# Linear attention with a mixture of experts: moving VectorE work behind the scaling of y, spreading attention to tile 129, and turning the rows of tiles 14 to 26 by transfers

## The chip, the cores and the metric

One core of a Trainium2 chip runs the whole kernel. TensorE (PE in the profile), VectorE (DVE), ScalarE (ACT), GpSimd (POOL) and SyncE (SP) each work through their own queue in order; SP, ScalarE and GpSimd also start DMA transfers. The metric is the device time of one execution in microseconds (us). Shown times are medians of several executions; the profile is of one execution.

## The reference, cut to what matters

x has 8 sequences of 1024 rows of 256 float32. The rows are layer-normalised (xn), and two things are added to x:

```
q = elu(xn @ Wq.T) + 1;  k = elu(xn @ Wk.T) + 1;  v = xn @ Wv.T        # 16 heads of 16
kv_cumsum = cumsum over rows of k outer v;  k_cumsum = cumsum over rows of k
out = (q . kv_cumsum) / clip(q . k_cumsum, 1e-6)                       # causal, per head
attention = out @ Wo.T

logits = xn @ Wr + br;  the best two of 8 experts, softmax over the two
ffn = sum over the two experts of weight * (silu(xn @ W1[e]) * (xn @ W3[e])) @ W2[e]

result = x + attention + ffn
```

W1 and W3 are 256 x 512 for each expert, W2 is 512 x 256. All arithmetic that goes to the result is float32.

## The kernel before, in words

**Two streams of work.** The 8192 rows are 16 blocks of 512 rows (`NBLK`), each of four chunks of 128. Attention goes block by block. The experts work on tiles of 128 gathered rows of one expert each: 132 tiles (`NM`), of which the first 25 (`N1`) come from lists made of the first four blocks (`FB`), the others from lists made of all blocks (`second_batch`). After a setup of some 47 us the main loop calls `tile_step(j)` for j = 0 to 132; each call does one expert tile and, spread between, a few steps of attention, normalisation, routing and list making.

**Order.** In the main loop only TensorE's order is written out by hand (`tc.manual_schedule(engines={EN.PE})`). What VectorE, ScalarE and GpSimd do next is set by the framework's planner when the kernel is built: it takes what it reckons to be ready, earlier program text first. `in_order` fixes the order of single instructions on their engine (the SP transfers, some ScalarE work), and `tc.issue_after(ins)` puts instructions of the same engine as `ins`, traced within it, behind `ins`.

**An expert tile** (`ffn_step`, line 1429). `ffn_weights(j + 2)` (line 1365) loads W1 and W3 of the tile two ahead, 512 KB each, on SP. `ffn_hidden(j)` (line 1378) multiplies by W1 (16 matmuls, called the gate here), calls `between`, multiplies by W3 (16 matmuls), then ScalarE applies silu and VectorE multiplies (hT). Then the rows of tile j + 1 are turned, then `ffn_out(j - 1)` (line 1405) does the 8 matmuls with W2 for the tile before, and VectorE scales the result by the routing weight into y (line 1417). `ffn_store` (line 1419) has GpSimd add y to the result rows by an indirect DMA. Such stores, and the accumulating transfers of attention (line 1099), read and write the output, so each waits for the landing of the one before.

**Turning rows.** Gathered rows (xg) are normalised by `ffn_norm` on ScalarE and must be transposed before the gate. Tiles below `TURNED` go through TensorE: `ffn_turn` (line 1344), two 128x128 transposes into PSUM and a ScalarE copy, one tile ahead. The others are normalised two tiles ahead; `ffn_halves` (line 1317, VectorE) splits the floats into 16-bit halves, `ffn_turn_halves` (line 1324) has SP start a transposing transfer between the two weight loads, and `ffn_join` (line 1334, ScalarE) puts the halves together, one tile ahead. Before, `TURNED` is 27.

**Attention.** `block_steps` (line 1106) is a generator with 8 steps a block: projections of k, q and v (0 to 2), divisors and the scores of chunk 0 (3), and one step for each chunk (4 to 7). In a chunk's step `attend` (line 1083) multiplies the last chunk's outcome (oT) by Wo, `carry` (line 1024) multiplies q by the running state, `scores` (line 1003) computes the next chunk's scores, which VectorE masks (line 1018), and `weigh` (line 1037) adds the scores' part and makes the new state: VectorE writes oT (line 1065), the new product (line 1068) and adds the old state (line 1077). `attend_upto(n)` (line 1145) advances the steps to n, of 129 (`LAST`); `upto` in `tile_step` says how far tile j may go. From tile 22 (`READ`) on it rises evenly, to reach 129 at tile 121 (`END`).

**Tiles 1 to 11 also prepare a block each** (block t = 4 + j). `turn(t)` (line 348) transposes block t between gate and W3; `logits(t)` follows the outputs. `normalise(t + 1)` (line 330, ScalarE, four activations) comes at the end of the tile in `finish`. It needs `stats` (line 298: VectorE, four pairs of operations on a block) and `deviations` (line 307: 17 small VectorE operations, each on the one before, for two blocks at a time). Both are called early in the tile, before `ffn_step`, two blocks ahead. Every fourth block `route` (line 417) chooses experts and counts (`counting`, tiles 4, 8 and 12; the counts are the matmuls of line 483).

**Tiles 14 to 21 also make the second lists**: in each, five calls `piece(0)` to `piece(4)` advance `second_batch` (line 741) by a `one_hot` (VectorE lines 606 and 619, ScalarE lines 624 and 626), four matmuls (line 771) and sums (line 780).

**PSUM.** y, the divisors, the outputs of `attend` and the lists' sums share two buffers (`ps_y`); scores, gate and W3 products share four (`ps_mm`).

Of the kernel before, what the change touches and what calls it, by code (L numbers as in the profile page):

```python
# [51 lines left out]
ALU = mybir.AluOpType  # L52
# [12 lines left out]
def tile_attention_moe(  # L65
# [14 lines left out]
    nc = tc.nc  # L80
# [5 lines left out]
    NCH = TB // P  # L86
# [7 lines left out]
    FB = 4  # L94
# [209 lines left out]
    def moments_tile(n):  # L304
        return f_two.tile([P, n * NCH, 2], F32, tag="mv", name="mv")
# [800 lines left out]
    def block_steps(t):  # L1106


        yield from project(t)
        denominators(t)  # L1110
        if t + 1 < NBLK:
            fetch(t + 1)
        waiting = scores(t, 0)
        if behind:
            attend(*behind.pop())
        yield
        done = None
        for c in range(NCH):
            if done:
                attend(*done)  # L1120
            both_ps = carry(t, c)
            coming = scores(t, c + 1) if c + 1 < NCH else None
            oT = weigh(both_ps, *waiting)
            done = t, c, oT
            waiting = coming
            yield
        behind.append(done)
        if t + 1 == NBLK:
            attend(*behind.pop())
            yield  # L1130
# [274 lines left out]
    def ffn_out(j, last=False):  # L1405
        hT = hs.pop(j)
        e = expert_of(j, mybir.EngineType.PE)
        y_ps = ps_y.tile([P, H], F32, tag="y", name="y_ps")
        for i in range(IC):
            done = nc.tensor.matmul(  # L1410
                y_ps, lhsT=hT[:, i, :], rhs=w2_sb[:, bass.ds(e * (IC * H) + i * H, H)],
                start=(i == 0), stop=(i == IC - 1),
            )
            if last:
                in_order(done)
        ys[j] = ffn5.tile([P, H], F32, tag="y", name="y")
        nc.vector.tensor_scalar(ys[j], y_ps, entry.pop(j)[:, 0:1], None, ALU.mult)  # L1417

    def ffn_store(j):
        _, _, _, _, rows, dst_i, i = of_tile(j)  # L1420
# [30 lines left out]
                stored[0] += 1  # L1451


    TURNED = 27
    gathered = ffn_load(0)
    with tc.issue_after(gathered.ins):
        in_order(nc.gpsimd.tensor_copy(te_late, batches[0][1]))
# [14 lines left out]
                nc.sync.dma_start(out=wo_sb, in_=woT.rearrange("(k p) o -> p k o", p=P))  # L1472
            )
    LATE = 3
    END = NM - 11
    LISTS = NBLK - FB
    READ = LISTS + 10
    AHEAD = 2 + LISTS // 2 + READ - LISTS
    held = {}

    def tile_step(j):
        nonlocal routing
# [8 lines left out]

        def piece(place):
            if LISTS + 2 <= j < READ or (j, place) == (READ, 0):
                next(held["lists"])

        def between():
            if turning:
# [14 lines left out]
        def finish():  # L1512
            if turning:
                held["lgT"] = f_two.tile([P, P], F32, tag="lgT", name="lgT")
                nc.scalar.copy(held["lgT"], logits(t))
            if counting:
                next(routing)
            if t + 1 < NBLK:
                normalise(t + 1)

        if LISTS <= j < LISTS + NBLK - FB:
# [3 lines left out]
        if j < LISTS:  # L1525
            upto = 3 + j // 2
        elif j < READ:
            upto = AHEAD - (READ - j - 1)
        else:
            upto = AHEAD + (LAST - AHEAD) * (j - READ + 1) // (END - READ + 1)  # L1530
        waits = attend_upto(upto, put_off=True)
        if t <= NBLK:
            with tc.issue_after((last_token if j < 3 else last_masked)[0].ins):
# [8 lines left out]
                if counting:  # L1542
                    routing = route(t - ROUND, t)
                    next(routing)
                of_blocks = [] if j == 0 else [t + 1, t + 2] if j == 1 else [t + 2]
                for a in of_blocks:
                    if a < NBLK:
                        if a % 2 == FB % 2:
                            held["mv"] = moments_tile(2)
                        some = slice(0, NCH) if a % 2 == FB % 2 else slice(NCH, 2 * NCH)  # L1550
                        stats(a, held["mv"][:, some])
                        if a % 2 != FB % 2:
                            deviations(a - 1, 2, held.pop("mv"))
        piece(1)
        ffn_step(j, LATE if N1 < j <= N1 + LATE else 0, between, after, late, finish)
        piece(4)
# [74 lines left out]
```

## Time and profile before

| | |
|---|---|
| median of 12 executions | 1249.22 us (1246.66 to 1253.48) |
| profiled execution, its own time | 1248.42 us |
| its span | 1246.7 us |
| TensorE busy | 1193.9 us (96%) |
| VectorE busy | 686.2 us (55%) |
| ScalarE busy | 588.5 us (47%) |
| GpSimd busy | 549.9 us (44%) |
| moved by DMA | 252.68 MB, mean 203 GB/s |
| transposing transfers of rows | 105 |

How to read it: "busy" is the time in which an engine carried out instructions; TensorE's has its pipelined matmuls modelled. A line such as `L1417 DVE ... y<-y_ps,entry` names the code line, the engine, what is written and what is read. "PEclk" is the TensorE clock that was granted, as a share of full speed. `xN` counts instructions. "idle before <-releaser" is how long the engine stood still before an instruction and whose end let it go; where several things were waited for, it is the last that the profile sees. In the table by stretches the columns are: the stretch, its length, then busy time and instruction count of PE, PE's weight loads, DVE, ACT and POOL, then PEclk, the DMA share and GB/s. In the table of waits the three figures are total us, number of times and the longest.

### The profile page before, as it was taken

The page shows a single profiled execution, that of the slowest core. Times are in us where ns is not written, and L with a number is a line of the kernel's source. Part 1 is how long each engine was busy: PE and PEld are TensorE (multiplying, and loading weights), DVE is VectorE, ACT ScalarE, POOL GpSimd, SP SyncE. Part 2 cuts the span into 40 slices and gives each one's busy share as a digit, 9 for nine tenths or more (in the row PEclk, how much of TensorE's full clock was granted, in tenths as well). Part 3 has the DMA queues.
Part 4 walks back from the last instruction along what each step waited for, and adds up shares of the span by engine and source line. Part 5 has one row for each costly group of instructions (what it writes and reads, how often), then busy time and mean ns, then how long its engine had stood idle before and what let it go on. Part 6 is the DMA issues. An engine that isn't in the chain of part 4 may idle for free. (4 is left out here: it accounts for less than half of the span.)

```text
span 1246.7 us, 29841 instructions
## 1 busy us (share of the span) xinstructions
PE 1193.9 (96%) x11394; PEld 1049.6 (84%) x11394; DVE 686.2 (55%) x1537; ACT 588.5 (47%) x1098; POOL 549.9 (44%) x474
## 2 busy tenths in 40 slices
PE   8799998899999999999999999999999999999992
PEld 6688887778989898989888889898988888888992
DVE  7866669755455555454555555555536464646320
ACT  5655576592363535352727262626272626262230
POOL 4734343325444544444444444444445444444342
PEclk9989999999999999999999999999999999999996
DMA  9898667557898988889898989898999798988992
GB/s 327 310 290 241 183 204 211 140 165 198 185 242 199 192 214 182 202 193 228 183 218 173 218 174 210 183 210 183 204 191 230 162 226 169 225 169 208 196 241 26
DMA packets 232463, 252.68 MB, mean 203 GB/s; under 512 B 101474, under 2 KB 156386, under 8 KB 232034
## 3 DMA queue, kind: packets, MB, share of 16 engines
q1 hardware_dynamic: 189298, 198.61, 56.8%
q0 software_dynamic: 38272, 43.22, 25.0%
q10 hardware_dynamic: 4752, 8.91, 2.1%
q8 instruction: 94, 1.54, 0.5%
q14 instruction: 47, 0.39, 0.1%
HBM read 187.91 MB, written 44.29 MB: 186 GB/s over the span
## 5 line engine op out<-in xcount | busy, mean ns | idle before, releaser
L1391 PE MATMUL gu_ps<-xgT,w 128*128 128x128 f32 x4224 | 505.7, 277 | 1.8 <-ACT xgT L1352 0.9
L1391 PEld LDWEIGHTS gu_ps<-xgT,w 128*128 128x128 f32 x4224 | 491.0, 193 | 17.2 <-issue 10.0
L1421 POOL DMA_INDIRECT out_dram<-y,dst_i x107 | 173.8, 1624 | 311.7 <-DVE s_sb L1018 76.6
L1410 PE MATMUL y_ps<-w_sb,hT 128*128 x1056 | 250.8, 380 | 1.7 <-DVE hT L1402 0.9
L1297 POOL DMA_INDIRECT xg<-in_x_dram,src_i x132 | 135.2, 1024 | 193.6 <-DVE half L1320 87.6
L1399 ACT ACTIVATE hT<-gu_ps 128x512 f32<-128x512 f32 x132 | 79.3, 601 | 290.6 <-PE gu_ps L1391 280.2
L1410 PEld LDWEIGHTS y_ps<-w_sb,hT 128*128 128x128 f32 x1056 | 190.4, 190 | 23.8 <-issue 1.8
L1018 DVE TENSOR_TENSOR s_sb<-s_ps,causal 128x512 f32<-128x512 f32 x256 | 158.3, 680 | 75.3 <-PE s_ps L1011 75.3
L1402 DVE TENSOR_TENSOR hT<-gu_ps,hT 128x512 f32<-128x512 f32 x132 | 90.4, 685 | 59.4 <-PE gu_ps L1391 43.6
L1302 POOL DMA_INDIRECT entry<-tab_d,of_i x107 | 108.6, 1015 | 32.6 <-issue 32.0
L1320 DVE COPY half<-xg 128x512 uint16<-128x512 uint16 x105 | 47.0, 447 | 133.4 <-ACT xg L1310 133.4
L1417 DVE TENSOR_SCALAR y<-y_ps,entry 128x256 f32<-128x256 f32 x132 | 63.6, 482 | 98.0 <-PE y_ps L1410 94.7
L1096 ACT COPY at<-a_ps 128x256 f32<-128x256 f32 x64 | 23.8, 372 | 167.6 <-PE a_ps L1091 167.6
L1310 ACT ACTIVATE xg<-xg,entry 128x256 f32<-128x256 f32 x132 | 79.0, 600 | 8.0 <-DMA entry<-tab_d,of_i 4.9
L1338 ACT COPY xgT<-halfT 128x512 uint16<-128x512 uint16 x105 | 80.2, 764 | 3.4 <-DMA halfT<-half 3.4
L1011 PE MATMUL s_ps<-qm,kT 32*128 32x256 f32 x1024 | 75.6, 408 | 0.0
L1091 PE MATMUL a_ps<-wo_sb,oT 128*128 128x256 f32 x256 | 68.1, 388 | 6.1 <-DVE oT L1065 4.1
L1421 POOL DMA_INDIRECT acc_d<-y,src_i x25 | 43.6, 1742 | 59.1 <-DVE y L1417 22.3
L1048 PE MATMUL o_ps<-s_sb,va 128*32 128x128 f32 x2048 | 69.4, 276 | 0.0
L1048 PEld LDWEIGHTS o_ps<-s_sb,va 128*32 128x32 f32 x2048 | 52.2, 110 | 18.2 <-issue 16.2
L1091 PEld LDWEIGHTS a_ps<-wo_sb,oT 128*128 128x128 f32 x256 | 46.1, 190 | 18.3 <-DVE oT L1065 5.1
L1099 POOL DMA_DIRECT2D out_dram<-at x27 | 35.9, 1328 | 56.0 <-DMA out_dram<-y,dst_i 21.9
(236 smaller groups left out, 1417.2 us busy)
## 6 DMA issues: line engine op xcount, KB each, us to landing
w<-in_w_dram SPq DMA_DIRECT2D x264, 512.0 KB
rden<-over SPq DMA_DIRECT2D x128, 64.0 KB
xnT<-xnT_d SPq DMA_DIRECT2D x15, 512.0 KB
out_dram<-at POOLq DMA_DIRECT2D x27, 256.0 KB
out_dram<-in_x_dram SPq DMA_DIRECT2D x12, 512.0 KB
xnT_d<-xnT ACTq DMA_DIRECT2D x11, 512.0 KB
xb<-in_x_dram SPq DMA_DIRECT2D x9, 512.0 KB
w_sb<-in_w_dram SPq DMA_DIRECT2D x4, 1024.0 KB
```

Of the source, the lines that this page charges most:

```text
L1018: last_masked[0] = nc.vector.tensor_tensor(sm, s_ps[r].rearrange("p k a l -> p (k a) l"), causal_b, ALU.mult)
L1048: nc.tensor.matmul(o_ps[32 * r : 32 * r + 32, hh, :], lhsT=va[:, c, 4 * hh + r, a, :], rhs=s_sb[r][:, 2 * hh + a, :], start=(first and a = ...
L1091: nc.tensor.matmul(a_ps, lhsT=oT[:, hh, :], rhs=wo_sb[:, hh, :], start=(hh == 0), stop=(hh == 1),)
L1297: rows = nc.gpsimd.indirect_dma_start(out=xg[j], out_offset=None, in_=x_rows[:, :], in_offset=bass.IndirectOffsetOnAxis(ap=src_i[:, i : i ...
L1302: nc.gpsimd.indirect_dma_start(out=entry[j], out_offset=None, in_=table[:, :], in_offset=bass.IndirectOffsetOnAxis(ap=num_i[:, i : i + 1], ...
L1310: nc.scalar.activation(xg[j], xg[j], AF.Identity, bias=entry[j][:, 1:2], scale=entry[j][:, 2:3])
L1338: nc.scalar.copy(xgT[j].bitcast(U16).rearrange("p k (l b) -> p b k l", b=2), halves.pop(j).rearrange("p (b k) l -> p b k l", b=2),)
L1391: done = nc.tensor.matmul(ps[:, i, :], lhsT=w13[:, k, bass.ts(i, P)], rhs=xgT[j][:, k, :], start=(k == 0), stop=(k == KC - 1),)
L1399: silu = nc.scalar.activation(hT, gu[0], AF.Silu)
L1402: nc.vector.tensor_tensor(hT, gu[1], hT, ALU.mult)
L1410: done = nc.tensor.matmul(y_ps, lhsT=hT[:, i, :], rhs=w2_sb[:, bass.ds(e * (IC * H) + i * H, H)], start=(i == 0), stop=(i == IC - 1),)
L1421: nc.gpsimd.indirect_dma_start(out=rows[:, :], out_offset=bass.IndirectOffsetOnAxis(ap=dst_i[:, i : i + 1], axis=0), in_=ys.pop(j), in_off ...
```

## The change

Four things are altered.

1. `TURNED` becomes 2 + 16 - 4 = 14: tiles 14 to 26 are turned by transposing transfers, as those from 27 on.
2. The VectorE instruction that scales y is kept in `held_y`. Every call that advances the second lists is put behind the latest one. So are the deviations, which move from before `ffn_step` to `finish` (tiles 1, 3, 5, 7, 9), and the statistics that used to be taken early in tiles 4 and 8 and the second of the two in tile 1; those move to `finish` as well. The other statistics stay early.
3. In a chunk's step `carry` comes before `attend`.
4. `upto` rises from tile 22 so as to reach 129 at tile 129 (`NM` - 3) instead of 121; `END` is gone.

```diff
         for c in range(NCH):
+            both_ps = carry(t, c)
             if done:
                 attend(*done)
-            both_ps = carry(t, c)
             coming = scores(t, c + 1) if c + 1 < NCH else None
...
-        nc.vector.tensor_scalar(ys[j], y_ps, entry.pop(j)[:, 0:1], None, ALU.mult)
+        held_y[0] = nc.vector.tensor_scalar(ys[j], y_ps, entry.pop(j)[:, 0:1], None, ALU.mult)
+
+    held_y = [None]
...
-    TURNED = 27
+    TURNED = 2 + NBLK - FB
...
-    END = NM - 11
...
+    def take_stats(t):
+        second = t % 2 != FB % 2
+        if not second:
+            held["mv"] = moments_tile(2)
+        stats(t, held["mv"][:, second * NCH : (second + 1) * NCH])
...
         def piece(place):
             if LISTS + 2 <= j < READ or (j, place) == (READ, 0):
-                next(held["lists"])
+                with tc.issue_after(held_y[0].ins):
+                    next(held["lists"])
...
             if t + 1 < NBLK:
+                if j > 0:
+                    with tc.issue_after(held_y[0].ins):
+                        if t + 2 < NBLK and (counting or j == 1):
+                            take_stats(t + 2)
+                        if t + 2 < NBLK and t % 2 != FB % 2:
+                            deviations(t + 1, 2, held.pop("mv"))
                 normalise(t + 1)
...
-            upto = AHEAD + (LAST - AHEAD) * (j - READ + 1) // (END - READ + 1)
+            upto = min(LAST, AHEAD + (LAST - AHEAD) * (j - READ + 1) // (NM - 2 - READ))
...
-                of_blocks = [] if j == 0 else [t + 1, t + 2] if j == 1 else [t + 2]
-                for a in of_blocks:
-                    if a < NBLK:
-                        if a % 2 == FB % 2:
-                            held["mv"] = moments_tile(2)
-                        some = slice(0, NCH) if a % 2 == FB % 2 else slice(NCH, 2 * NCH)
-                        stats(a, held["mv"][:, some])
-                        if a % 2 != FB % 2:
-                            deviations(a - 1, 2, held.pop("mv"))
+                if t + 2 < NBLK and j > 0 and not counting:
+                    take_stats(t + 1 if j == 1 else t + 2)
```

## The prediction

> **What bounds the kernel now.** I read the page first: engine shares, then the 40 slices.
>
> ```profile
> PE 1193.9 (96%) x11394; PEld 1049.6 (84%) x11394; DVE 686.2 (55%) x1537; ACT 588.5 (47%) x1098; POOL 549.9 (44%) x474
> ...
> PE   8799998899999999999999999999999999999992
> ```
>
> TensorE is busy without a break from about 300 us to 1225 us at a granted clock of 1.00; there only removed matmuls help. Time can come from two other places: the waits before 300 us, and the last slice. The waits of TensorE, longest in total first:
>
> ```profile
> PE den L980 <- DVE y L1417: 4.8, 2, 3.6
> PE a_ps L1091 <- DVE oT L1065: 4.1, 3, 2.6
> PE cnt_ps L483 <- DVE mv L302: 3.7, 2, 2.0
> PE a_ps L1091 <- DVE y L1417: 1.9, 2, 1.0
> ```
>
> Each is VectorE doing something else first (block statistics, list pieces). Some cost more than their length. In the table by stretches (TensorE busy is the second figure, the granted clock the third from the end) the stretch after the 2.01 us wait at 134.6 has clock 0.59, the one after the 2.64 us wait at 219.7 has 0.72:
>
> ```profile
> 56.00:60.00 4.00, 3.29 (x33) 2.53 (x32) 4.00 (x26) 0.64 (x2) 2.41 (x3) 1.00 1.08 364
> ...
> 135.00:137.00 2.00, 2.00 (x11) 1.93 (x11) 1.70 (x11) 1.68 (x2) 1.70 (x2) 0.59 0.33 39
> ...
> 220.00:226.00 6.00, 6.00 (x82) 4.70 (x81) 3.23 (x7) 0.79 (x2) 1.77 (x2) 0.72 0.22 27
> ```
>
> The timeline of the end shows the second place: the last output is scaled at 1225.45, but GpSimd still owes four stores, one after another:
>
> ```profile
> 1225.45 0.48 DVE L1417 TENSOR_SCALAR y<-y_ps,entry 128x256 f32<-128x256 f32 x1 [2.09 <-PE y_ps L1410]
> 1225.71 1.55 POOL L1421 DMA_INDIRECT out_dram<-y,dst_i  x1 [3.89 <-issue]
> 1230.22 1.55 POOL L1421 DMA_INDIRECT out_dram<-y,dst_i  x1 [2.96 <-issue]
> 1234.81 1.55 POOL L1421 DMA_INDIRECT out_dram<-y,dst_i  x1 [3.04 <-DMA out_dram<-y,dst_i]
> 1239.32 1.55 POOL L1421 DMA_INDIRECT out_dram<-y,dst_i  x1 [2.96 <-issue]
> ```
>
> The span ends at 1246.7, 21.2 us after that scaling. Stores into the output wait for each other.
>
> **A. Rows of tiles 14 to 26 turned by transfers.** Removed: 13 pairs of transposes. A pair costs TensorE the time from its start to the next matmul's:
>
> ```profile
> 302.82 0.38 PE L1348 MATMUL xg_t<-ident,xg 128*128 128x128 f32 x2
> ...
> 303.04 1.89 PE L1410 MATMUL y_ps<-w_sb,hT 128*128 x8
> ```
>
> 0.22 us, so 13 x 0.22 = 2.9 us gained. Moved: ScalarE joins (0.764) instead of copying (0.365), 0.40 more per tile, 5.2 in all; VectorE gets a split copy of 0.447 each, 5.8 in all; SP issues 13 transposes of 1.2 to 2.1 us between the two weight loads of a tile. Cover: a transfer starts two tiles ahead, some 20 us, and weights come as early. The cover is thinnest for tile 25: its expert is known only when the lists are done, and after the score-divisor transfers its weight loads leave SP at 300.18 with four more behind them, while its first matmul runs at 309.61. How slow a transpose can be in such a crowd, the trace shows once:
>
> ```profile
> 332.46 1.45 SPq L1329 DMA_TRANSPOSE halfT<-half  x1
> ...
> 343.15 0.77 ACT L1338 COPY xgT<-halfT 128x512 uint16<-128x512 uint16 x1 [3.44 <-DMA halfT<-half]
> ```
>
> 10.7 us. Issued near 301.5, tile 25's would land between 304 and 312 and be joined 0.8 later: loss 0 to 3, taken 1. The VectorE and ScalarE cover in the list tiles is counted in C. A: +1.9 (range -0.5 to +3).
>
> A rule stands against this part. The Trainium skill ("VectorE: DVE Perf Modes", section "Rules for kernel authors") says to turn a 128x128 block on TensorE where PSUM will do, and by DMA otherwise; its section "The three transpose paths" has 390 ns against 1309 ns. If that difference were paid in full for 13 tiles (an estimate from these two figures: 12 us), the total below would become about 6 us slower than before. The trace's rows price TensorE at 0.11 us per turned block and show 105 later tiles whose transfers made it wait 0.3 us once, so I go by the rows.
>
> **B. Statistics and deviations (tiles 1 to 11).** In tiles 4 and 8, where routing runs, a block's statistics (4 x 0.57 = 2.3 us) move behind the scaling of y; in tiles 1, 3, 5, 7, 9 the chain of deviations (17 dependent operations, 0.2 us apart, 3.4 us) does. Gained: the waits of the counts, 1.65 in tile 4 and 2.01 in tile 8; behind the latter 16 gate matmuls took 3.30 instead of 1.95 and five others 0.6 longer, so 3.9 together; two waits for logits behind a late y, 1.3. Sum +6.9. The 3.58 us before the divisors of tile 2 I count as nothing: VectorE is busy 4.00 of 4.00 us there, its work stays, and the wait moves to the gate matmuls or the turn of block 6.
>
> What is late next: normalising a block (2.08 on ScalarE) needs the deviations, and TensorE turns it after the next tile's gate matmuls, with the whole in-order queue (second half, outputs) behind. From the scaling of y: 0.4 + 3.4 + 2.1 = 5.9 us. From there to the turn the trace has 127.25 - 121.04 = 6.2 in tile 8 and 108.08 - 101.87 = 6.2 in tile 6 (just enough; 0.8 for both, as the masking of scores, 4 x 0.62, starts to interleave), 149.03 - 143.90 = 5.1 in tile 10 (short by 0.8, with interleaving 1.4), 87.20 - 82.58 = 4.6 in tile 4 (short by 1.3; the masks are ready 1.6 us after y and, taken in between, add 2.5; I take 3 and 1 for the clock). Tile 2: 0.5. Sum -6.7. B: 0. Bounds: no interleaving and tile 2 gaining 1.3 gives +6; interleaving everywhere, the clock falling in two tiles, -8.
>
> The Trainium skill ("TensorE: Matmul & The Clock Gate", section "HAM oscillation — how this bites in real kernels") warns only of idle gaps longer than 3.4 us. By that rule the 2.01 us gap would cost itself alone and B would come to -0.9; the row has clock 0.59 after it.
>
> **C. List pieces behind y, carry before attend (tiles 14 to 22).** VectorE scales y 0.9 to 1.2 us earlier. The waits it holds: 1.19 (divisors), 0.97 (list fill), 2 x 0.97 (outputs); of these 3.8 go, also because the carried product (0.61) now fills the wait for the free PSUM buffer. In tile 17 TensorE waits 2.64 for oT; y and oT could come 1.9 earlier, but the product that now goes first needs the new state, two operations (0.84) later: +1.5 with the clock. Against it: the next list piece starts after y, so its matmuls can wait on VectorE and ScalarE (2 x 1.25 of pieces behind 2.42 of masks): I take 2.5 once; and the 0.45 + 0.40 per tile from A fall where VectorE is busy 11.4 of 12 and ScalarE 26.4 of 29 us: 1.3, plus 0.5 for the 1.48 wait on ScalarE that is there now. C: +1.0. Bounds: all 9.2 us of waits there gone but 3, +6; every tile paying 0.6 for the order, -5. From tile 23 on the state is ready long before the next step, and the swapped order costs nothing; if it were not, 0.84 per step.
>
> **D. Attention up to tile 129.** TensorE's work is the same and it never idles, so its end does not move by this. What moves is the chain of stores. Call T the start of the tile with the last two steps: 1159.9 now (tile 121), tile 129 then. Around T one output store leaves at T - 7.8, then an accumulation, an output, the last accumulation, and the outputs of tiles 128 to 131. Start-to-start times: an output store beside weight loads 5.6 to 6.8 (1181.83 to 1206.70), without them 4.5; an accumulation 9.6 (1157.82) and 6.5 (1175.33); the last store to the end 7.4. After T + 8 no weights are left to load, so 5.8 + 9.6 + 4.6 + 5.3 + 3 x 4.5 + 7.4 = 46.2, ending at T + 38.4. The last scaling: gate of 129 at T + 4.2, two tiles of 5.3, then 8.35 as now: T + 23.2. So 15.2 instead of 21.2: +6.0. Bounds: loaded prices throughout, 53.8, gives -1.6; 6.5 for the first accumulation and 4.5 to 5 for the rest, +9.5.
>
> **Sum.** 1.9 + 0 + 1.0 + 6.0 = 8.9 us. The profiled execution took 1248.4 (span 1246.7), 0.8 below the median of 1249.2; against the median: 1240.
>
> **Rivals.** (1) *The stores catch up and VectorE's waits go without new ones.* For it: in the middle the store mostly waits for y, not for a landing. With no backlog the end comes 8.2 after the last scaling, 13 gained; with 2.9 and 2: 1231. Against it: two accumulations in the last two tiles. (2) *Slower: the late normalisation.* If the interleaved masks hold up the chain in all five turning tiles, each pays 2.5 and the clock 1.9, as after 134.6; from three such tiles (13.2) beyond my count the gain is eaten: 1249.2 - 8.9 + 13.2 = 1253.5. It decides from 2.3 us per tile over five. For it: tile 4 has no slack; against it: tiles 6 and 8 just fit. (3) *The end only shifts.* If the backlog stays 21 us and tile 25's transpose lands late, 2.9 - 2 + 0 + 1 is left: 1247 to 1249, no change.
>
> **Chances.** Forecast (4 to 12 gained: 1237 to 1245) 0.46; (1) 0.20; (3) 0.13; (2) 0.21. 0.2% is 2.5 us, about what a measurement of this kernel can tell from none. Faster 0.66, same 0.13, slower 0.21. Range 1231 (rival 1, also A, B, C and D near their upper ends) to 1254 (rival 2).
>
> **What would show it.** Right: 13 pairs fewer of L1348; no wait of the counts in tile 8; fewer than three stores after the last scaling; end within 17 us of it. Wrong: a wait of the block transposes (L357) for ScalarE above 4 us in a tile; a wait of the gate matmuls of tile 25 or 26 for the join; a list matmul (L771) waiting over 3 us; VectorE's order in the later tiles so changed that TensorE idles after 310 us, which it does not now.

## The result and the profile after

The changed kernel takes 1262.27 us (median of 9 runs, 1260.28 to 1267.17), the kernel before 1248.75 in the same comparison (37 runs). The ratio is 1.0113, 95% interval 1.0098 to 1.0128: 1.1% slower, 14 us. I had predicted 1240, with 1254 as the upper end. The profiled execution has a span of 1260.0 us.

The page of the changed kernel, TensorE's total, its 40 slices and the granted clock:

```profile
PE 1200.0 (95%) x11368; PEld 1045.3 (83%) x11368; DVE 693.0 (55%) x1550; ACT 592.0 (47%) x1098; POOL 554.2 (44%) x474
...
PE   8889997878999999999999999999999999999996
...
PEclk9989999888999999999999999999999999999998
```

A slice is 31.5 us. The seventh to tenth digit (189 to 315 us) have gone to 7 and 8, with a lowered clock in the last three of them, while the last slice has gone from 2 to 6: the end is better, the middle much worse. The waits of TensorE in the changed kernel (total us, times, longest):

```profile
PE gu_ps L1391 <- ACT xgT L1338: 14.7, 6, 4.2
PE held_ps L771 <- ACT parts L626: 5.2, 4, 2.4
PE tp L357 <- ACT xb L340: 4.3, 3, 4.0
PE o_ps L1030 <- DVE kv L1077: 3.8, 1, 3.8
PE gu_ps L1391 <- DVE s_sb L1018: 3.6, 4, 1.7
```

In the kernel before, the same two groups of matmuls waited for ScalarE much less:

```profile
PE held_ps L771 <- ACT parts L626: 1.7, 2, 1.5
...
PE gu_ps L1391 <- ACT xgT L1352: 0.9, 2, 0.5
```

So the first line of the changed kernel is new in size: the gate's matmuls wait for the join of the turned rows, in tiles 18 to 23. The waits of the counts for the moments, which B was to remove, are gone. To see where time is lost I follow the start of the scaling of y (line 1417) tile by tile, after minus before. It is +2.8 to +4.2 in tiles 1 to 7 and back to -0.34 in tile 12; then it grows: 5.16 (tile 15), 11.57 (18), 23.31 (20), 25.08 (24) and still 25.09 (28). Tile j is scaled in the step of tile j + 1, so nearly all of the loss lies in the eight steps that make the second lists (14 to 21). From tile 12 to tile 24 it is 25.4 us, a good deal more than the 14 that are left at the end: the shorter end gives some 10 back.

Tile 19 shows how. First ScalarE's timeline, then TensorE's, of the changed kernel (start, length, engine, line, what; in brackets the idle time before and who ended it):

```profile
253.84 0.37 ACT L1096 COPY at<-a_ps 128x256 f32<-128x256 f32 x1 [4.14 <-PE a_ps L1091]
254.20 0.66 ACT L624 ACTIVATE parts<-held,row 128x440 bf16<-128x440 bf16 x1
254.76 0.83 ACT L626 ACTIVATE parts<-held 128x110 bf16<-128x110 bf16 x4
255.50 0.65 ACT L624 ACTIVATE parts<-held,row 128x440 bf16<-128x440 bf16 x1
256.05 0.83 ACT L626 ACTIVATE parts<-held 128x110 bf16<-128x110 bf16 x4
256.79 0.65 ACT L624 ACTIVATE parts<-held,row 128x440 bf16<-128x440 bf16 x1
257.34 0.83 ACT L626 ACTIVATE parts<-held 128x110 bf16<-128x110 bf16 x4
258.08 0.74 ACT L1338 COPY xgT<-halfT 128x512 uint16<-128x512 uint16 x1
```

```profile
255.09 0.81 PE L771 MATMUL held_ps<-parts,at_place 128*128 128x220 bf16 x4 [0.28 <-ACT parts L626]
258.88 2.76 PE L1391 MATMUL gu_ps<-xgT,w 128*128 128x128 f32 x16 [2.98 <-ACT xgT L1338]
...
275.25 3.79 PE L1391 MATMUL gu_ps<-xgT,w 128*128 128x128 f32 x16 [4.15 <-ACT xgT L1338]
```

ScalarE works its queue in order. The join (258.08) stands behind three groups of list pieces, and behind a copy for which ScalarE had stood idle 4.14 us; the transfer it needs left SP at 233.36. The join itself never waited for a transfer, as the page's group of it says (busy us, mean ns, idle us before):

```profile
L1338 ACT COPY xgT<-halfT 128x512 uint16<-128x512 uint16 x118 | 90.0, 763 | 0.0
```

So the rows were there, and the instruction that hands them on was late in its queue. In the kernel before, the copy of turned rows (here those of tile 20, in the step of tile 19) stands among the list pieces:

```profile
252.62 0.66 ACT L624 ACTIVATE parts<-held,row 128x440 bf16<-128x440 bf16 x1 [0.68 <-PE held_ps L771]
253.19 0.35 ACT L1352 COPY xgT<-xg_t 128x256 f32<-128x256 f32 x1
```

Every such wait is paid twice: 16 gate matmuls, 1.96 us elsewhere, take 2.76 after the wait of 2.98 and 3.79 after that of 4.15, and the 16 W3 matmuls behind them still take 2.59 and 2.43. The table by stretches shows the clock of it (third figure from the end; between the same times the kernel before has 0.91 and 1.00):

```profile
220.00:240.00 20.00, 16.19 (x136) 13.35 (x137) 10.95 (x23) 8.69 (x29) 3.92 (x3) 0.77 0.43 134
...
260.00:280.00 20.00, 15.85 (x87) 14.46 (x86) 8.41 (x16) 12.55 (x31) 1.94 (x1) 0.76 0.43 100
```

At the end, as forecast, stores no longer pile up:

```profile
1247.38 1.55 POOL L1423 DMA_INDIRECT out_dram<-y,dst_i  x1 [2.97 <-DMA out_dram<-y,dst_i]
1248.54 0.48 DVE L1417 TENSOR_SCALAR y<-y_ps,entry 128x256 f32<-128x256 f32 x1 [2.09 <-PE y_ps L1410]
1252.86 1.56 POOL L1423 DMA_INDIRECT out_dram<-y,dst_i  x1 [3.92 <-issue]
```

One store starts after the last scaling instead of four, and the span ends 11.5 us after it instead of 21.2.

### The profile page after: what moved, and what is told of

Same layout as the page of the kernel before. It is cut to its first block, busy times and chain, and to the rows that moved or that the text cites. A ratio compares the mean times of both kernels' runs of the same rounds, so it can differ in the third digit from the quotient of the medians.

```text
span 1260.0 us, 29797 instructions
## 1 busy us (share of the span) xinstructions
PE 1200.0 (95%) x11368; PEld 1045.3 (83%) x11368; DVE 693.0 (55%) x1550; ACT 592.0 (47%) x1098; POOL 554.2 (44%) x474
## 4 chain that ended last, share of the span: by engine, by line
PE 85%; DVE 7%; ACT 4%; DMA 3%; issue 1%; POOL 0%; POOLq 0%; SPq 0%; ACTq 0%; DVEq 0%
PE gu_ps L1391 36%; PE y_ps L1410 17%; PE s_ps L1011 5%; PE o_ps L1048 5%; PE a_ps L1091 4%; PE zkk L863 4%; PE zkv L863 4%; PE zq L842 4%; PE o_ps L1030 2%; PE tp L357 1%; DVE s_sb L1018 1%; DMA out_dram<-y,dst_i 1%; PE held_ps L771 1%; DMA wr_sb<-in_wr_dram 1%; PE den L980 1%
## 5 line engine op out<-in xcount | busy, mean ns | idle before, releaser
L1391 PE MATMUL gu_ps<-xgT,w 128*128 128x128 f32 x4224 | 511.8, 279 | 19.2 <-ACT xgT L1338 14.7
L1320 DVE COPY half<-xg 128x512 uint16<-128x512 uint16 x118 | 52.6, 446 | 130.6 <-ACT xg L1310 129.8
L1096 ACT COPY at<-a_ps 128x256 f32<-128x256 f32 x64 | 23.8, 372 | 207.7 <-PE a_ps L1091 207.7
L1338 ACT COPY xgT<-halfT 128x512 uint16<-128x512 uint16 x118 | 90.0, 763 | 0.0
L1011 PEld LDWEIGHTS s_ps<-qm,kT 32*128 32x128 f32 x1024 | 46.7, 186 | 19.1 <-issue 16.6
```

Source lines behind the costliest of these rows:

```text
L1011: nc.tensor.matmul(s_ps[r][:, hh].rearrange("p a l -> p (a l)"), lhsT=kT[rows, hh, span], rhs=qm[rows, hh, :, span], start=True, stop=True,)
L1338: nc.scalar.copy(xgT[j].bitcast(U16).rearrange("p k (l b) -> p b k l", b=2), halves.pop(j).rearrange("p (b k) l -> p b k l", b=2),)
L1391: done = nc.tensor.matmul(ps[:, i, :], lhsT=w13[:, k, bass.ts(i, P)], rhs=xgT[j][:, k, :], start=(k == 0), stop=(k == KC - 1),)
```

## The experiments

The runs came in series of two speeds: the kernel before took 1248 us in some and 1276 to 1277 in others. The number of the chip does not tell them apart (chip 4 is in both), so what makes the difference is not known. Results are therefore ratios to the kernel before in the same series. The changed kernel, b3, a5, a3 and b4 below belong to the 1248 kind, all others to the 1276 kind; a comparison across the two kinds takes it that ratios carry over, which holds only roughly. "Delay" below is how much the lateness of the scaling of y grows from tile 12 to tile 24, against a reference of the same kind: the kernel before on the 1248 kind, attention alone (b1) on the 1276 kind, where the kernel before has no profile. For the changed kernel it is 25.4 us.

### Which part costs: one part alone, and one part undone

Attention to tile 129 alone (called b1 from here):

```diff
-            upto = AHEAD + (LAST - AHEAD) * (j - READ + 1) // (END - READ + 1)
+            upto = min(LAST, AHEAD + (LAST - AHEAD) * (j - READ + 1) // (NM - 2 - READ))
```

> The kernel before with one line changed: attention is spread up to tile 129. Nothing else. From the last scaling to the end the changed kernel took 11.5 us against 21.2 before. If that is this line's work alone: 9 to 10 us faster, 1238 to 1241, with the first 300 us as before within 1 us. Rival, the shorter end comes partly from the 24 us by which the changed kernel's stream was late (the stores had more time): the gain is only 3 to 6 us, 1243 to 1246.

Measured: 0.9941 (0.9924 to 0.9957), that is 7.4 us of 1248. The end was 11.6 us after the last scaling, as in the changed kernel. The prediction had 6 us for it; the 9 to 10 expected above were too many, the rival's 3 to 6 too few.

The turns alone, in the kernel before (b2):

```diff
-    TURNED = 27
+    TURNED = 2 + NBLK - FB
```

> The kernel before with one line changed: rows from tile 14 on turned by transfers. Theory 1 (the join's place on ScalarE behind the list pieces): the loss of tiles 13 to 20 appears here alone, 12 to 22 us, 1261 to 1271, with waits of the gate's matmuls for the join of 3 us and more. Rival (the carry and the list order cause it): within 3 us of the kernel before, 1246 to 1252.

Measured: 1.0091 (1.0069 to 1.0113), delay 12.5 us, and the gate waits 12.1 us for the join, five times, at most 4.0. At 1248 us this ratio is 11.4 us, just under the 12 expected. The turns cost by themselves, with the old order of everything else.

The changed kernel with the turns undone (a1):

```diff
-    TURNED = 2 + NBLK - FB
+    TURNED = 27
```

> The changed kernel with the rows of tiles 14 to 26 turned by TensorE again; statistics behind the outputs, the list pieces and the carry as changed, and attention up to tile 129 stay. Theory 1 (the join of the turned rows on ScalarE stands behind three or four groups of list pieces of 1.5 us each, TensorE waits for it and then runs at a lowered clock): the waits of the gate's matmuls for the join are gone, 15 to 22 of the 24.5 us that tiles 13 to 20 lost come back, the granted clock of 230 to 300 us rises from 0.86 to 0.95 or more, time 1240 to 1247. Rival (the carry ahead of the attention and the later place of the list pieces are the cause): tiles 13 to 20 lose as before, 1256 to 1262.

Measured: 1.0053 (1.0034 to 1.0073), 0.6% better than the changed kernel, but slower than before although the end gains 0.59%. Delay 6.1. So theory 1 is not the whole: something else costs too. Its rival, the carry and the list pieces, has a share. The next runs took the parts away one after another.

Statistics and deviations with b1, nothing else (b3):

> The kernel before with attention up to tile 129 and with the statistics and deviations of tiles 1 to 11 behind the outputs; TensorE turns up to tile 26, list pieces and carry as before. Against the run with attention alone (0.59% faster than before): if the first tiles' loss that the changed kernel shows (2.9 to 4.2 us in tiles 1 to 7, 0.1 to 0.6 from tile 8 on, on the first chip; 5 to 6 on the second) remains, it is 0.2 to 0.5% faster than before; if it is taken back by the end of tile 12, 0.55 to 0.75% faster.

Measured: 0.9940 (0.9917 to 0.9963), the same ratio as b1, though b1 is of the other kind. B is worth nothing here: of its 3.4 to 4.7 us of loss in tiles 1 to 7 all but 1.1 is back by tile 12.

List pieces behind the outputs in addition (a5); it is the changed kernel with the turns and the carry undone:

```diff
-            both_ps = carry(t, c)
             if done:
                 attend(*done)
+            both_ps = carry(t, c)
```

> The changed kernel with TensorE turning up to tile 26 and with the attention of a chunk ahead of the carry as before; what is left is the list pieces behind the outputs, the statistics behind the outputs and attention up to 129. With the carry ahead as well it was 0.53% slower than before. If the carry's wait for the state (3.8 us in the changed kernel) and the slower clock after it are the cost: 0 to 0.3% faster than before. If the list pieces behind the outputs are (waits of list matmuls for parts, 6.8 us there against 1.7): 0.3 to 0.5% slower.

Measured: 0.9993 (0.9976 to 1.0011). From 0.9940 the list pieces' later place has cost 0.53%, 6.6 us; delay 6.9. TensorE's timeline of this run, then the lines of ScalarE's that it waits on:

```profile
272.45 1.96 PE L1391 MATMUL gu_ps<-xgT,w 128*128 128x128 f32 x16
278.56 0.81 PE L771 MATMUL held_ps<-parts,at_place 128*128 128x220 bf16 x4 [4.15 <-ACT parts L626]
279.21 3.52 PE L1391 MATMUL gu_ps<-xgT,w 128*128 128x128 f32 x16
```

```profile
270.50 0.66 ACT L624 ACTIVATE parts<-held,row 128x440 bf16<-128x440 bf16 x1 [2.92 <-DVE held L619]
...
275.79 2.54 ACT L852 ACTIVATE qm<-qT,par 128x512 f32<-128x512 f32 x4
278.23 0.83 ACT L626 ACTIVATE parts<-held 128x110 bf16<-128x110 bf16 x4
```

VectorE begins a list piece only after y, so ScalarE stands idle 2.92 us, and its share of the next pieces falls behind the projections' work and the masked q. TensorE's list matmuls, in order ahead of the W3 matmuls, wait 4.15 us, and the 16 W3 matmuls then take 3.52 us instead of 1.96.

The carry, first alone with b1 (c1) and then in the changed kernel without turns and with the old list order (a6; statistics, carry and attention are left):

> The kernel before with attention up to tile 129 and the carry ahead of the attention of the chunk before; nothing else. The runs with and without the carry ahead came from two chips, and differ by 0.6%. If the carry ahead costs that by itself (it waits up to 3.8 us for the state and TensorE runs slower after it): 0 to 0.2% faster than before. If the 0.6% is the chip's (there the first tiles lost 5 us, here none): 0.45 to 0.7% faster.

> The changed kernel with TensorE turning up to tile 26 and with the list pieces no longer put behind the outputs; left are the statistics, the carry ahead and attention up to 129. If the list pieces' later place is the one other cost beside the turns (0.53% between two runs): 0.45 to 0.7% faster than before, no list matmul waiting over 2 us for parts. If the carry matters in their company: under 0.3% faster.

Measured: 0.9946 (0.9923 to 0.9969) and 0.9994 (0.9972 to 1.0017). Both delays are about 0 (-0.4 and 0.0), though in both TensorE does wait 3.6 us for the state. The swap of carry and attention costs nothing: it trades one wait for another. What separates the two is the first tiles: on this kind the statistics behind the outputs lose 7.6 us against b1 by tile 1, and 5.6 are left at the end; on the other kind nearly all is won back. So a6 misses the 0.45 to 0.7% expected, and that is most of why a1, from the 1276 kind, looked worse than a5. Against a6, a1 gives the list order a second measure: 0.59%.

The changed kernel with only the list order undone (a10):

```diff
-                with tc.issue_after(held_y[0].ins):
-                    next(held["lists"])
+                next(held["lists"])
```

> The changed kernel with one thing undone: list pieces not put behind the outputs. Turns by transfer from tile 14, carry ahead, statistics and attention as changed. If turns and list pieces add up (turn alone 0.91% slower than before, attention alone 0.59% faster): 0.2 to 0.5% slower than before. If they hinder each other: 0 to 0.2% slower or faster. If the pieces' place cost only without the turns: 0.9 to 1.2% slower.

Measured: 1.0063 (1.0035 to 1.0092), delay 17.2. Against the run without turns (a6) that is 0.69%, 8.6 us of 1248, for the turns; it is a little more than the 0.2 to 0.5% expected if the parts add up, since the statistics cost on this kind. The delays add up, within what the two kinds allow: 17.2 (turns, no list order) and 6.9 (list order, no turns) make 24.1, the changed kernel has 25.4.

### Why the turns cost: place, load or transfer

The changed kernel with list pieces not ahead of the newest join (a2; `held_join` keeps the join's instruction):

```diff
-                with tc.issue_after(held_y[0].ins):
+                with ExitStack() as behind_both:
+                    behind_both.enter_context(tc.issue_after(held_y[0].ins))
+                    if held_join[0]:
+                        behind_both.enter_context(tc.issue_after(held_join[0].ins))
                     next(held["lists"])
```

> The changed kernel with its turned rows, in which a list piece may also not be put ahead of the newest join in the planner's order. Theory 1: the matmuls of the gate wait less than 1.5 us for the join in each list tile (before up to 4.2), and at least half of the 24.5 us comes back: 1243 to 1252. Rival, transfers that land late: the wait stays as long, since the join itself waits for the transfers: 1257 to 1263. Rival, too much work for ScalarE and VectorE in the list tiles (0.40 and 0.45 us per tile): the waits move from the join to other ScalarE or VectorE results and the time stays within 4 us of 1262.

Measured: 1.0133 (1.0100 to 1.0166), no gain. TensorE's waits from 190 to 330 us:

```profile
PE held_ps L771 <- ACT parts L626: 13.9, 8, 3.9
PE o_ps L1030 <- DVE kv L1077: 3.8, 1, 3.8
PE gu_ps L1392 <- ACT xgT L1337: 2.5, 2, 1.4
```

The join's wait fell from 14.7 to 2.5, and the list matmuls' wait for ScalarE rose from 5.2 to 13.9: the wait went from one customer of ScalarE to the other. This is what the rival named above for too much work on ScalarE and VectorE, so the load has to be tested by itself. In this run's timeline the join stands right behind the projections' work (276.43), and the list pieces now behind the join. So this run leaves two readings open: too much work, or a place that stays late although the pair is in order.

Is it ScalarE's and VectorE's load? b1 with the turned rows' extra instructions in tiles 12 to 24, read by nobody (d1):

```diff
+        if 12 <= j < 25:
+            spare = ffn2.tile([P, 2, H], U16, tag="half", name="spare")
+            nc.vector.tensor_copy(
+                spare, xg[j + 1].bitcast(U16).rearrange("p (h b) -> p b h", b=2)
+            )
+            spared = ffn2.tile([P, H], U16, tag="halfT", name="spared")
+            nc.scalar.copy(spared, spare[:, 0, :])
```

> The kernel before with attention up to tile 129 (0.59% faster than before by itself), rows turned by TensorE up to tile 26, and in tiles 12 to 24 two more instructions that nobody reads: VectorE splits the next rows as for a transfer, and ScalarE copies 128x256 halves. That is the extra work of the turned rows (about 0.45 us VectorE, 0.4 us ScalarE a tile) without transfers and without anyone waiting. If the extra work itself fills ScalarE or VectorE in the list tiles: 3 us or more of the 0.59% are lost, 0 to 0.35% faster. If only place and waiting cost: 0.45 to 0.7% faster.

Measured: 0.9923 (0.9897 to 0.9950), nothing lost against b1. Its delay is 3.6 us, in tiles 21 and 22, and is won back later. With the old list order, the extra work as such is not the price; with the list pieces behind the outputs it was not tested alone.

Is it ScalarE? The changed kernel with the joins of rows 14 to 26 on VectorE (a4), where the planner puts them behind other work too:

```diff
-            nc.scalar.copy(
+            (nc.vector.tensor_copy if j < 27 else nc.scalar.copy)(
```

> The changed kernel with the joins of rows 14 to 26 made by VectorE instead of ScalarE. In the order that the planner makes, the join now stands behind the projections' work and list pieces of VectorE as it stood behind those of ScalarE. If the place that the planner gives it is the cause, whatever the engine: the gate still waits 6 us or more in all for the join, 0.7 to 1.1% slower than before. If ScalarE's load is the cause: 0.1 to 0.5% slower, and the gate's waits are under 3 us.

Measured: 1.0199 (1.0160 to 1.0237), worse. Delay 33.1. Two joins in VectorE's timeline, then the gates behind them in TensorE's:

```profile
256.05 0.45 DVE L1338 COPY xgT<-halfT 128x512 uint16<-128x512 uint16 x1
...
286.67 0.45 DVE L1338 COPY xgT<-halfT 128x512 uint16<-128x512 uint16 x1
```

```profile
256.60 3.75 PE L1391 MATMUL gu_ps<-xgT,w 128*128 128x128 f32 x16 [2.77 <-issue]
...
287.22 3.76 PE L1391 MATMUL gu_ps<-xgT,w 128*128 128x128 f32 x16 [3.43 <-issue]
```

The gate starts 0.1 us after the join each time, though the profile calls the wait "issue" (13.9 us in all) and names the join only once (2.1). A shorter join (0.45 against 0.75) on an engine with other work does not help: neither ScalarE as such nor the length of the join is the cause.

Where does the late place come from? My guess was that the planner sets a join where it takes the transfer to have landed. So the rows up to 24 were normalised and sent three tiles ahead instead of two:

```diff
-        if TURNED <= j + 2 < NM:
-            ffn_norm(j + 2)
-            ffn_halves(j + 2)
+        for a in [j + 3] if j + 3 < N1 else [j + 2]:
+            if TURNED <= a < NM and a not in normed:
+                normed.add(a)
+                ffn_norm(a)
+                ffn_halves(a)
...
-            if s == 0 and halved and j >= TURNED:
-                ffn_turn_halves(j)
+            a = j + 1 if j + 1 < N1 else j
+            if s == 0 and halved and a >= TURNED and a not in sent:
+                sent.add(a)
+                ffn_turn_halves(a)
```

The rows are also gathered a tile earlier, and the turned halves (`halfT`) have three buffers. The first two runs have only one buffer for the split halves (`half`); the later ones have two, and `mine` in the list code has one less. First in the changed kernel (a3), then in b1 (b4):

> The changed kernel, with the rows of tiles 14 to 24 normalised, split and sent into their transposing transfer one tile earlier (three ahead instead of two), so that the planner knows the joined rows as ready sooner and places the join ahead of the projections' ScalarE work. Times against the kernel before on the same chip. Theory 1b (what costs is the place of the join on ScalarE, and the late landing that the planner assumes makes that place): the gate's waits for the join fall from 14.7 us to under 4, the list matmuls' waits for parts stay near 5, 6 to 12 us come back against the changed kernel: 0.2 to 0.7% slower than before. Rival, the list tiles simply lack ScalarE time for the join: the waits only move to parts as in the run with the join first, and it stays 1.0 to 1.4% slower.

> The kernel before with attention up to tile 129, rows from tile 14 on turned by transfers, and these sent one tile earlier as in the run above; statistics, list pieces and carry as before. Against the kernel before: turning from tile 14 alone was 0.91% slower and attention up to 129 alone 0.59% faster, so without the earlier transfers I expect about 0.3 to 0.4% slower. Theory 1b: 0.3 to 0.7% faster. Rival, lack of ScalarE time: 0.1 to 0.5% slower.

Measured: 1.0668 (1.0631 to 1.0705) and 1.0504 (1.0460 to 1.0548), far slower, and by my own doing: the one buffer. From tile 25 on VectorE waited for it:

```profile
DVE half L1323 <- DMA halfT<-half: 129.6, 23, 13.8
```

But up to tile 24 the two runs answer part of the question. The changed kernel and a3 have the same list order and are of the same kind. The join of the rows of tile 20 stands behind the projections' work (L810, L809) in the changed kernel, and ahead of it in a3:

```profile
273.94 0.62 ACT L810 ACTIVATE neg<-neg 128x512 f32<-128x512 f32 x1
274.46 0.75 ACT L1338 COPY xgT<-halfT 128x512 uint16<-128x512 uint16 x1
```

```profile
261.11 0.75 ACT L1341 COPY xgT<-halfT 128x512 uint16<-128x512 uint16 x1
...
266.67 0.57 ACT L809 ACTIVATE neg<-zkk 128x512 f32<-128x512 f32 x1
```

What waits of TensorE are left in a3 between 180 and 330 us:

```profile
PE held_ps L771 <- ACT parts L626: 9.3, 6, 4.1
PE o_ps L1030 <- DVE kv L1077: 5.4, 1, 5.4
...
PE gu_ps L1396 <- ACT xgT L1341: 1.0, 1, 1.0
```

The wait for the join falls from 14.7 to 1.0 us, and the delay from 25.4 to 15.1. Of the 18.5 us that the turns make with this list order (25.4 less the 6.9 of a5), 10.3 come back. The other 8.2 do not: the waits of the list matmuls rise from 5.2 to 9.3 and that for the state from 3.8 to 5.4, so the rival of too little time on ScalarE is partly right here, or at least not excluded. With the old list order, b4's gates wait 1.0 us for the join too, its join of tile 20 (252.94) is ahead of the projections' work (257.59), and its delay is only 0.5 us; the turns alone with the late place (b2, of the other kind) made 12.5. The work and the engine are the same and no join of the changed kernel had waited for its transfer, so an earlier landing by itself could gain nothing: what changed for the gates is the place.

### What is left, and the best version

The same with two buffers, in the changed kernel (a9) and in b1 (b5):

> The changed kernel with earlier transfers for rows 14 to 24, as in the run before that sent them earlier, but with two buffers for the split halves instead of one (from tile 26 on that run waited 129.6 us for the one buffer). Times against the kernel before on the same chip. Up to tile 24 that run had 10 us less delay than the changed kernel; if it was the buffer alone that cost the rest, the stream from tile 25 on keeps 14 to 15 us of delay and the time is 0.2 to 0.5% slower than before (the changed kernel: 1.13%). If the earlier transfers themselves harm the later tiles: slower than 1%.

> The kernel before with attention up to tile 129, rows turned by transfers from tile 14 on, and these transfers a tile earlier with two buffers for the halves. Attention alone was 0.59% faster. If the join's late place was the whole cost of the turns, and TensorE now saves its 2.9 us for 13 tiles: 0.6 to 0.9% faster than before. If some cost of the turns is left in the list tiles: 0.2 to 0.6% faster.

Measured: 1.0078 (1.0052 to 1.0105) and 1.0005 (0.9981 to 1.0030). The waits for the buffer are gone, and the later loss with them. No gate waits for a join in either run between 180 and 330 us. The first is better than the changed kernel's 1.0113, though less than the 0.2 to 0.5% I had expected: its delay is 19.8 us, not 14 to 15, with list matmuls waiting 7.5 us for ScalarE and 6.2 us of waiting for the state. With the list order the earlier transfer thus cures the gates' waits and not the whole loss (a1, without turns, has a delay of 6.1). The second falls short by 0.6% and its delay is 8.6 us, most of it in tiles 21 and 22. There ScalarE waits for the gathered rows of tile 25, whose addresses the lists have only just made:

```profile
298.34 0.60 ACT L1311 ACTIVATE xg<-xg,entry 128x256 f32<-128x256 f32 x1 [4.49 <-DMA xg<-in_x_dram,src_i]
```

In b5, rows 25 and 26 by TensorE again, which are normalised one tile later (c2; `by_transfer` leaves out 25 and 26 and replaces the comparisons with `TURNED`):

```diff
+    def by_transfer(j):
+        return TURNED <= j < NM and j not in (25, 26)
```

> The kernel before with attention up to tile 129, earlier transfers for rows 14 to 24 with two buffers for the halves, and rows 25 and 26 turned by TensorE as before. With rows 25 and 26 by transfer as well it was as fast as before (1.0005), and ScalarE waited 4.5 us for the gathered rows of tile 25, with 7 to 8 us lost in tiles 21 and 22. If that wait is what is left of the turns' cost: 0.5 to 0.9% faster than before. If the extra work in tiles 21 and 22 is: 0 to 0.3% faster.

Measured: 0.9963 (0.9940 to 0.9986), between the two expectations; delay 3.3, as much as the extra work alone had (3.6). That would put the wait for the gathered rows at 5 us of b5's delay; the next pair of runs, which is written the same up to tile 22, makes it less.

Attention one tile later still (130), in b5 (b6) and in c2 (c3):

```diff
-(NM - 2 - READ))
+(NM - 1 - READ))
```

> As the run with the two buffers and old lists, attention reaching its last step one tile later (130). If the stores at the end still wait for each other there (11.5 us from the last scaling to the end), a tile more of spreading gives 0 to 3 us: 0.6 to 1.1% faster than before. If the last block's accumulating transfer then comes behind the last outputs, it costs 2 to 5 us: 0.2 to 0.6% faster.

> The run above with attention reaching its last step one tile later (130). The same pair without it differed by 0.46%, in favour of 130, with intervals that touch. If the later end itself is worth that: 0.3 to 0.5% faster than the run above. If it is the executions' spread: within 0.2% of the run above.

Measured: 0.9959 (0.9935 to 0.9984) and 0.9949 (0.9925 to 0.9973). Against 129 the first is 0.46% better, with intervals that touch, and the second 0.14%, well within them: no difference is shown. The delays are 6.7 and 5.5 us, so with and without the transfers of rows 25 and 26 they differ by 5.2 us in one pair (b5, c2) and by 1.2 in the other (b6, c3), and the times by 0.42% and 0.10%. What the wait for the gathered rows costs lies between, and is not shown more closely.

None of the versions with earlier turns is faster than the last part of the change by itself. That one line (b1), 0.59% faster than the kernel before, beats both kernels.

## Why the prediction was wrong

The parts in us at 1248 us (gain positive; "kind" is that of the series):

| part | predicted | measured | from |
|---|---|---|---|
| A, turns by transfer | +1.9 (-0.5 to +3) | -15.0; -8.6 on the 1276 kind | changed 1.0113 against a5 0.9993 (the carry is worth nothing); a10 1.0063 against a6 0.9994, old list order |
| B, statistics and deviations | 0 (-8 to +6) | 0; -6.0 on the 1276 kind | b3 0.9940 (1248 kind) against b1 0.9941 (1276 kind); a6 0.9994 against c1 0.9946 |
| C, list pieces and carry | +1.0 (-5 to +6) | -6.6 and 0; list pieces -7.4 on the 1276 kind | a5 0.9993 against b3; c1 0.9946 against b1; a1 1.0053 against a6 |
| D, attention to 129 | +6.0 (-1.6 to +9.5) | +7.4 | b1 0.9941 (1276 kind) |

The measured terms of the first column of figures sum to -14.2; the change itself, by its ratio, is -14.1. That they agree is no proof: before, b3, a5 and the changed kernel are one chain of runs, and the terms are its steps.

**A failed, and it is the step "Cover: a transfer starts two tiles ahead, some 20 us".** The transfer was covered (none of the 118 joins waited for one); what follows it was not. The turns were forecast to gain 1.9 us and cost 15.0. I priced the join by its length (0.40 more per tile) and put that into C, and never asked where in ScalarE's queue it would stand. In the kernel before, the copy of the turned rows depends on TensorE's transposes just before it, and the planner sets it among the list pieces (253.19 in tile 19). The join depends on a transfer, which the planner, it seems, takes to be late, and stands behind other work; the gates waited 14.7 us for it. That place accounts for the gates' waits and for 10.3 of the 18.5 us of delay that the turns make (a3); how the other 8.2 divide between work and order on ScalarE stays open. The 105 later tiles that wait "0.3 us once", on which I relied, say nothing on this: they lie outside the tiles that make lists, so no list pieces stand in ScalarE's queue there. The rivals missed it as well: none had the gate matmuls of tiles 18 to 23 waiting. The sign I named was right in kind (a gate wait for the join), but set for tiles 25 and 26, where the changed kernel has none. The thin cover at tile 25 that I had priced at 1 us exists, though for the gathered rows and not for the transpose, and showed only once the stream was early again: 4.5 us of waiting on ScalarE in b5.

I had set aside the Trainium skill ("VectorE: DVE Perf Modes", sections "Rules for kernel authors" and "The three transpose paths"), which prefers TensorE for turning such a block; by its two durations, paid in full, I had worked out an estimate of a total 6 us slower. The runs side with the rule's preference in this stage, but not with a price taken from the durations. The longer path was not what TensorE waited for: no join of the changed kernel waited for a transfer, and with the transfers a tile earlier b4 loses 0.5 us up to tile 24.

**C had the mechanism and not the size.** "The next list piece starts after y, so its matmuls can wait on VectorE and ScalarE" is what happens; I took 2.5 us once. Without the turns (a5) the list matmuls wait 9.4 us in all between 180 and 330 us (6.8 for ScalarE, 1.4 and 1.2 for VectorE), where in b1 they wait 1.9, and behind the longest the next 16 matmuls take 3.52 us instead of 1.96. The gain on y's side came (the waits for oT, y and divisors fell), the price was larger. The swapped carry trades a wait for oT (3.6 us in b1) for one for the state (3.6 in a6) and is neutral.

**B was right as a sum on the 1248 kind, partly by luck.** The late normalisation came where 0.5 us had been put down for it: in tile 2 the turn of the block (L357) waits 4.0 us for ScalarE, in the changed kernel and in b3, as the prediction had said that the 3.58 us of waiting there would only move; b3 is 3.5 us behind after it. In tiles 4, 6, 8 and 10, for which 6.2 us of loss were counted, such a wait is at most 0.2 us. The gain in tile 8 came (3.3 us). On the 1276 kind the loss stayed, 6.0 us.

**D was right**, a little too small: the last scaling to the end took 11.5 us, not 15.2, and only one store was left.

On the clock I had weighed the Trainium skill's page "TensorE: Matmul & The Clock Gate" (section "HAM oscillation — how this bites in real kernels"), which warns of gaps longer than 3.4 us. Here again a shorter gap cost: after 2.98 us of waiting 16 matmuls took 2.76 instead of 1.96.

What stays open: on the 1276 kind part of a delay at tile 24 is won back between tiles 28 and 60 (a10: from 22.5 to 16.7 us against b1). On the 1248 kind nearly all is kept: against b3, which has the same attention, the changed kernel is 25.4 us late at tile 24 and still 23.8 at the last scaling. TensorE is busy 295.8 of 300 us from 600 to 900 in b1 and 299.99 in the changed kernel, so only the first has idle time in which a delay can shrink. I did not find what makes the two kinds differ. Nor was the landing of a transfer seen directly; that the planner's assumption places the join is concluded from the order that changes when the transfer is sent earlier.

## What to carry to other kernels

When work moves from TensorE to a transfer, follow the whole chain to the first matmul that needs it, and ask of each in-order queue on the way (here the join on ScalarE) what stands ahead of it, not only how long the instruction is. A steady state that hides a step proves nothing for a stage in which that step's engine has a full queue. And when a wait is forced away by order, look who takes it: here (a2) the wait for the join fell from 14.7 to 2.5 us and that of the list matmuls rose from 5.2 to 13.9.

## What the runs showed of the hardware

- A wait of 2.98 us of TensorE was followed by 16 matmuls at 2.76 us instead of 1.96, one of 4.15 by 3.79: in these 16 alone the gaps cost again a quarter to almost a half of their length.
- Series of runs differ: the same kernel before took 1248 us in some and 1276 to 1277 in others, 2.2%, and one part of the change (statistics behind the outputs) was worth nothing in the one kind (b3) and cost about 0.5% in the other (a6 against c1). The cause is not known.
- One buffer too few for a transfer's source cost 5 to 6% over a hundred tiles (b4 against b5, a3 against a9, by ratio): the engine that fills it waited 129.6 us in a3, up to 13.8 us at a time, for the transfer that reads it. The runs compared also differ in the kind and in one buffer of the list code.
- The profile can put a wait down to "issue" although a VectorE instruction ended 0.1 us before it did (five gate groups, 13.9 us).
